# Unread matmuls in the planned gaps of TensorE behind the last scores of layer 2

## The chip, the cores and the metric

The kernel runs on one core of a Trainium2 chip. A core has TensorE (PE, matmuls; its weight loads are listed as PEld), VectorE (DVE), ScalarE (ACT), GpSimd (POOL), SyncE (SP, which here only issues DMAs) and 16 DMA engines. The metric is the device time of one execution in microseconds; lower is better. Everything is float32.

## The reference

Four layers are applied one after the other to x (4 sequences of 512 tokens, 256 channels). All four attend to the same context of 512 tokens.

```python
x = _L0_xattn_ref(x, ctx_1024, mask, ...)   # a Mamba-2 block, then cross attention, 8 heads of 32
x = _L1_xattn_ref(x, ctx_1024, ...)         # cross attention, 8 heads of 16, then an MLP
x = _L2_xattn_ref(x, ctx_1024, ...)         # layer norm, cross attention, 16 heads of 16, GELU
x = _L3_xattn_ref(x, ctx_1024, ...)         # cross attention, 8 heads of 32, then a recurrence
```

What ends the kernel is the recurrence of layer 3, which runs over all 512 tokens in order, for the four sequences at once:

```python
    U = (xn @ W_in.T + b_in) @ Bmat
    def step(s, u_t):
        s = jax.nn.silu(s @ A.T) + u_t          # s: 4 x 64
        return (s, s)
    _, states = jax.lax.scan(step, zeros, U.transpose(1, 0, 2))
    x = residual + einsum('tbs,sh->bth', states, Cmat)
```

## The kernel before

**Tiles.** The 512 tokens are cut into four tiles c = 0 to 3 of 128. A tile goes through layers 0, 1, 2 and 3, then through its 128 steps of the recurrence. Tiles overlap: while the recurrence of one runs, the attention of later tiles fills the engines. Layers 0 and 3 are the "wide" stream (tiles `kw`, `vw`, `probs_w`, `turned_w`), layers 1 and 2 the "slim" one (`ks`, `vs`, `probs_s`, `topped`). `slim_second` makes the last scores of layers 1 and 2 and their exponentials; when its loop over jobs ends, layers 1 and 2 have no scores left.

**Order.** No compiler orders the work. Each piece is a Python generator that yields operations, and `Flow.run` emits the one that can begin first by a table of estimated costs, in nanoseconds. `Engine.free` is when the plan has an engine free, `Flow.there(ops)` when the operands are there, `account` writes down ends of writes and reads. `Flow.emit` emits one operation, and `Flow.rows` the scores of up to two heads' groups in turns. The plan's times are not the chip's: an engine executes in the order emitted and waits on semaphores. All operations are emitted by one helper, so the profile gives line 119 for all of them.

**PSUM.** The tile `ps` has eight banks of 512 columns. `Banks.single` names the free bank that was read longest ago and does not reserve it; users take it out of the free set themselves. The recurrence owns bank 7 (`z`).

**The recurrence.** For each tile, one product puts the inputs into bank 7 (`u` by `amat`, 512 columns). Then every step adds the product of the previous result with `amat` (or `ahalf`, half of it) and reads it:

```python
            for t in range(P):
                if last is not None:
                    yield mm(z[:, t, :], last[0], last[1], False, True, skip_group_check=True)
                zt = z[0:SD, t, :]
                if exps["left"] == 0:
                    yield A.activation(r[0:SD, t, :], zt, AF.Silu)
                    last = amat, r[:, t, :]
```

The product has 65 rows, 65 weight columns (SZ = 65) and 4 streamed columns. A float32 matmul shows as two weight loads and two passes; a transpose as one. While exponentials are left (`exps["left"]`), a step takes two operations, a tanh on ScalarE and a multiply on VectorE; afterwards one SiLU on ScalarE, and ScalarE loads another table for it once. `output` multiplies the states by `cmat` (68 rows, 256 columns, once per sequence) and adds them to `h`. For the last tile it sends the result out one sequence at a time.

Of the kernel before, what the change touches and what calls it, by code (L numbers as in the profile page):

```python
# [28 lines left out]
SZ = SD + 1  # L29
# [14 lines left out]
def over(ap, n):  # L44

    p, a = ap.shape
    return ap.unsqueeze(1).to_broadcast([p, n, a])
# [8 lines left out]
DRAIN = 95.0  # L56
NEAR = 120.0
BOOST = 0.4
APART = 150.0
ALONE = 1500.0  # L60
WAIT = 400.0
# [23 lines left out]
class Op:  # L85
    def __init__(self, engine, name, args, kw):
        self.engine, self.name, self.args, self.kw = engine, name, args, kw
        outs = [kw["out"]] if "out" in kw else [args[0]]
        ins = list(args if "out" in kw else args[1:])
        ins += [v for k, v in kw.items() if k not in ("out", "accum_out")]  # L90
        ins = [v for v in ins if isinstance(v, bass.AP)]
        if kw.get("accum_out") is not None:
            outs.append(kw["accum_out"])
        self.writes = [b for ap in outs for b in blocks(ap)]
        self.reads = [b for ap in ins for b in blocks(ap)]
        self.size = max(elements(ap) for ap in outs + ins)
        self.mode = None
        self.table = None
        if engine.kind == "PE":
            lhs = kw.get("lhsT", ins[0])  # L100
            self.mode = tuple(next(m for m in (32, 64, 128) if n <= m)
                              for n in (lhs.shape[0], outs[0].shape[0]))
            n = max(elements(outs[0]), elements(lhs))
            self.cost = n / 1.2 * (1 if name == "transpose" else 2) + 5
        elif engine.kind == "DVE":
            each = {"reciprocal": 8.0, "scalar_tensor_tensor": 1.3}.get(name, 1.05)
            self.cost = 150 + self.size * each
        elif engine.kind == "ACT":
            self.cost = 165 + self.size * 0.83 + (190 if "accum_out" in kw else 0)
            f = args[2] if len(args) > 2 else None  # L110
            if f is not None and f not in NO_TABLE:
                self.table = f if f in OTHER_TABLE else "exp"
        elif engine.kind == "POOL":
            self.cost = 1000 if ALU.pow in args else 100 + self.size * 2.1
        else:
            self.cost = 500

    def emit(self):
        return getattr(self.engine.bass, self.name)(*self.args, **self.kw)  # L119
# [57 lines left out]
class Banks:  # L177
# [9 lines left out]
    def pair(self):  # L187
# [3 lines left out]
            two, default=None,  # L191
            key=lambda p: (max(self.at(p), self.flow.now) + APART * (p[1] > p[0] + 1), p),
        )

    def single(self):

        def key(i):
            beside = len({i - 1, i + 1} & self.free)
            return (max(self.at((i,)), self.flow.now) + APART * beside, i)

# [20 lines left out]
class Flow:  # L221
    def __init__(self):
        self.written, self.read = {}, {}
        self.threads = []
        self.now = 0.0
        self.landed = [0.0] * 8
        self.bus = 0.0

    def add(self, steps, urgency, name=""):
        th = Thread(steps, urgency, name)  # L230
# [67 lines left out]
    def account(self, ops, start, end):  # L298
        for op in ops:
# [3 lines left out]
            for b in op.reads:  # L303
                self.read[b] = max(end, self.read.get(b, 0.0))

    def emit(self, ops):

        for op in ops:
            e = op.engine
            start = max(e.free, self.there([op]))  # L310
            cost = op.cost
            if e.kind == "PE" and e.mode != op.mode:
                start, e.mode = start + DRAIN, op.mode
            if op.table is not None and e.table != op.table:
                cost, e.table = cost + TABLE, op.table
            end = start + cost
            e.free = end
            if e.kind == "DMA":
                start = max(start, min(self.landed))
                e.free = start + cost  # L320
                self.bus = max(self.bus, start + 2000) + op.size * P * 4 / 300
                self.landed[self.landed.index(min(self.landed))] = end = self.bus
            op.emit()
            self.account([op], start, end)

    def rows(self, threads, start):
        e = threads[0].choices[0][0].engine
        if e.mode != (32, 128):
            e.mode = (32, 128)
        built = []  # L330
        for th in threads:
            th.banks = th.request.take()
            th.request.banks.free -= set(th.banks)
            built.append(th.request.build(th.banks))
            start = max(start, th.request.banks.at(th.banks))
        for r in range(max(len(b) for b in built)):
            rounds = [b[r] for b in built if r < len(b)]
            for j in range(len(rounds[0])):
                for rnd in rounds:
                    rnd[j].emit()  # L340
        e.free = start + max(ROWS[t.request.kind] for t in threads)
        for b in built:
            self.account([op for rnd in b for op in rnd], start, e.free)
# [70 lines left out]
def tile_kernel(ctx: ExitStack, tc: tile.TileContext, a: dict, out: bass.AP):  # L414
# [6 lines left out]
    flow = Flow()  # L421
# [7 lines left out]
    def new(pool, name, *shape, dtype=F32):  # L429
        return pool.tile(list(shape), dtype, tag=name, name=name)  # L430
# [4 lines left out]
    def mm(dst, lhsT, rhs, start=True, stop=True, **kw):  # L435
        return T.matmul(dst, lhsT=lhsT, rhs=rhs, start=start, stop=stop, **kw)
# [23 lines left out]
    ps = new(ctx.enter_context(tc.tile_pool(name="ps", bufs=1, space=PSUM)), "ps", P, 8, S)  # L460
    banks = Banks(flow, ps.name, range(8))
# [47 lines left out]
    ident = new(common, "ident", P, P)  # L509
# [988 lines left out]
    def press(job, urgency):  # L1498
# [4 lines left out]
        if c == lead and not (l == 3 and rest):  # L1503
            urgency -= BOOST
        elif l == 0 and c > lead + 1:
# [120 lines left out]
    slim = Stream([], "s")  # L1626
# [48 lines left out]
    def slim_second(lo):  # L1675

        for i in range(slim.all):
            yield Until(lambda: len(slim_base) > i + 1)
            job = slim.order[i]
            for s in range(KL[job["l"]]):  # L1680
                n = slim_base[i] + s
                yield Until(lambda: n // 2 in slim_q2)
                p = yield take(f"probs_s{lo}")
                press(job, SECOND)
                q2, k = slim_q2[n // 2], job["k"][s // 2]
                pr = yield Row("second", (lo, lo + 1), banks, lambda pr: [
                    [
                        mm(
                            ps[:, pr[g], t * P : (t + 1) * P],
                            group(k[:, s % 2, t * P : (t + 1) * P], lo + g),  # L1690
                            group(q2[0][:, n % 2, :], lo + g),
                        )
                        for g in range(2)
                    ]
                    for t in range(NT)
                ])
                q2[1] -= 1
                if q2[1] == 0:
                    rings["topped"].give(q2[0])
                yield from read_both(pr, lambda i, sc: A.activation(p[:, i, :], sc, AF.Exp))  # L1700
                slim_probs[n, lo] = p
            slim.keys_read(job)

    def slim_weigh():

# [20 lines left out]
    def slim_finish(job, slot, c):  # L1726

        n = KL[job["l"]]
        r = wide_tops["rs", job["b"]]
        bank = yield on_bank(lambda bank: [  # L1730
            tr(ps[:, bank, j * P : (j + 1) * P], c[:, j, :]) for j in range(n)
        ])
        pt = ps[:, bank[0], 0 : n * P].rearrange("p (j t) -> p j t", j=n)
        yield V.reciprocal(
            r[:, 0 : 4 * n], pt.rearrange("p j (g r) -> p (j g) r", r=G)[:, :, 16]
        )
        banks.give(*bank)
        rb = yield take("rb")
        yield G_.tensor_copy(rb[:, 0 : 4 * n, :], along(r[:, 0 : 4 * n], G))
        ct_slot = yield take("ct")  # L1740
        ct = ct_slot[:, 0:n, :]
        bank = yield on_bank(lambda bank: [
            tr(
                ps[:, bank, j * P : (j + 1) * P],
                rb[:, 4 * j : 4 * j + 4, :].rearrange("p h r -> p (h r)"),
            )
            for j in range(n)
        ])
        pt = ps[:, bank[0], 0 : n * P].rearrange("p (j t) -> p j t", j=n)
        rings["rb"].give(rb)  # L1750
        yield V.tensor_tensor(ct, c, pt, ALU.mult)
        banks.give(*bank)
        rings["c"].give(slot)
        flow.add(job["after"](job["c"], job["b"], ct_slot, ct), CHAIN, f"from {job['l']} {job['c']}")


    def with_keys_made():
# [147 lines left out]
```

## Time and profile before

| what | value |
|---|---|
| median of 3 runs | 1499.82 us (1499.3 to 1504.79) |
| profiled execution | 1498.61 us, span 1496.9 us |
| PE busy | 1385.8 us (93%) |
| PEld busy | 998.1 us (67%) |
| DVE busy | 942.4 us (63%) |
| ACT busy | 759.7 us (51%) |
| granted clock of TensorE, mean | 0.933 |
| 1300.0 to 1370.0 us: PE busy, clock | 64.05 us, 0.88 |
| 1370.0 to 1380.3 us: PE busy, clock | 8.25 us, 0.67 |
| 1380.3 to 1486.6 us: PE busy, ACT busy, clock | 67.49 us, 26.54 us, 0.50 |
| 1486.6 to 1496.9 us: PE busy, clock | 4.88 us, 0.50 |

The page cuts the span into 40 slices of about 37 us and gives each engine's busy share in tenths; PEclk is the clock that TensorE was granted, in tenths of full speed. A row of the timeline has the start in us, the duration in us, the engine, the operation with its tiles (output, then inputs), its shape and how many instructions were merged; the bracket gives the idle time before it and what ended it. A row of a stretch has, after the stretch and its length, busy microseconds and instruction counts for PE, PEld, DVE, ACT and POOL, then the clock, then the share and rate of the DMA. Busy times of TensorE overlap and have modelled ends: they contain the time in which a result travels through the array.

### The profile page before, as it was taken

How to read it: one execution, taken by the hardware profiler on the slowest of the kernel's cores; microseconds unless marked ns; L12 is line 12 of the kernel's file. 1: busy time of each engine (PE TensorE's matmuls, PEld its weight loads, DVE VectorE, ACT ScalarE, POOL GpSimd, SP SyncE). 2: the span in 40 equal slices, each digit the busy share in tenths (PEclk: the TensorE clock that was granted, in tenths of full speed). 3: DMA queues.
4: the chain of work that ended last, by engine and by line, in shares of the span. 5: the costliest groups of instructions: out<-in, count | busy, mean ns of one | idle time of the engine just before them, and what ended most of it. 6: DMA issues, size and time to landing. Idle time of an engine off the chain costs nothing.

```text
span 1496.9 us, 34529 instructions
## 1 busy us (share of the span) xinstructions
PE 1385.8 (93%) x14432; PEld 998.1 (67%) x14432; DVE 942.4 (63%) x2079; ACT 759.7 (51%) x1904; POOL 257.2 (17%) x403
## 2 busy tenths in 40 slices
PE   7999998998999999999999999999999999998665
PEld 5667675675676667776767777676777666776443
DVE  5885878644866765687666767766676666655000
ACT  4643443332654565766456666454576544555221
POOL 2355555652010010100010100001100000010000
PEclk9999999997999999999999999998999999988555
DMA  7412011114432121233112122221222212010000
GB/s 226 138 43 87 29 53 29 65 59 134 141 102 85 63 74 52 97 100 103 60 61 74 52 94 94 68 88 46 75 80 82 84 61 89 11 48 1 14 1 14
DMA packets 48467, 107.59 MB, mean 72 GB/s; under 512 B 13044, under 2 KB 24760, under 8 KB 48312
## 3 DMA queue, kind: packets, MB, share of 16 engines
q1 hardware_dynamic: 46808, 105.32, 21.3%
q8 instruction: 113, 1.85, 0.5%
q10 hardware_dynamic: 1504, 0.07, 0.1%
q14 instruction: 42, 0.34, 0.1%
HBM read 85.01 MB, written 20.37 MB: 70 GB/s over the span
## 4 chain that ended last, share of the span: by engine, by line
PE 78%; DVE 10%; ACT 7%; issue 3%; DMA 1%; POOL 1%; SPq 0%; DVEq 0%; ACTq 0%; POOLq 0%
PE ps L119 78%; DVE tops L119 3%; ACT rec L119 2%; ACT probs_s L119 2%; DVE xbc L119 1%; DVE top L119 1%; DVE stats L119 1%; ACT xt L119 1%; DVE dt L119 1%; DVE probs_w L119 1%; DVE xt L119 1%; ACT probs_w L119 1%; ACT L119 1%; DMA w_out<-in_L_xattn_out_proj_w 0%; DMA ctx_in<-in_ctx 0%
## 5 line engine op out<-in xcount | busy, mean ns | idle before, releaser
L119 DVE TENSOR_REDUCE tops<-ps 128x2 f32<-128x1024 f32 (+1 forms) x214 | 235.0, 1107 | 68.6 <-PE ps L119 67.7
L119 ACT ACTIVATE probs_s<-ps 128x1024 f32<-128x1024 f32 (+1 forms) x210 | 193.6, 948 | 98.2 <-PE ps L119 93.5
L119 PE MATMUL ps<-ks,queries 32*128 32x512 f32 x768 | 197.1, 652 | 9.5 <-DVE tops L119 4.4
L119 PE MATMUL ps<-topped,ks 32*128 32x128 f32 x3072 | 183.2, 289 | 5.5 <-DVE rec L119 2.3
L119 PEld LDWEIGHTS ps<-topped,ks 32*128 32x128 f32 x3072 | 151.4, 190 | 31.6 <-issue 11.3
L119 PEld LDWEIGHTS ps<-rec,ahalf 65*65 65x65 f32 x694 | 76.6, 140 | 102.1 <-DVE rec L119 35.8
L119 PE MATMUL ps<-ident,probs_w 128*128 128x128 f32 x1024 | 139.6, 283 | 1.6 <-DVE tops L119 0.7
L119 PEld LDWEIGHTS ps<-ident,probs_w 128*128 128x128 f32 x1024 | 117.8, 146 | 17.7 <-issue 7.6
L119 ACT ACTIVATE rec_th<-ps 64x4 f32<-64x4 f32 x347 | 56.8, 164 | 139.8 <-PE ps L119 137.3
L119 PE MATMUL ps<-kw,queries 32*128 32x512 f32 x512 | 116.3, 644 | 3.3 <-ACT rec_th L119 1.0
L119 ACT COPY turned_w<-ps 128x512 f32<-128x512 f32 x154 | 86.9, 584 | 49.9 <-PE ps L119 39.7
L119 PE MATMUL ps<-probs_s,vs 128*32 128x128 f32 x3072 | 107.7, 282 | 0.7 <-DVE tops L119 0.4
L119 PE MATMUL ps<-rec,ahalf 65*65 65x4 f32 x694 | 93.4, 205 | 8.4 <-DVE rec L119 7.8
L119 ACT ACTIVATE probs_w<-ps,top 128x512 f32<-128x512 f32 x128 | 87.0, 683 | 23.5 <-DVE top L119 22.6
L119 PE MATMUL ps<-rec,amat 65*65 65x4 f32 x328 | 61.9, 259 | 39.8 <-ACT rec L119 39.8
L119 ACT ACTIVATE probs_w<-probs_w,top 128x512 f32<-128x512 f32 x128 | 91.4, 718 | 13.3 <-DVE top L119 13.3
L119 DVE CUSTOM_DVE_ANT_0 probs_w<-ps,masked 128x512 f32<-128x512 f32 x128 | 84.6, 682 | 18.4 <-PE ps L119 18.3
L119 PEld LDWEIGHTS ps<-probs_s,vs 128*32 128x32 f32 x3072 | 80.8, 112 | 17.7 <-issue 7.5
L119 DVE TENSOR_REDUCE top<-ps 128x2 f32<-128x1024 f32 (+1 forms) x70 | 78.4, 1127 | 19.8 <-PE ps L119 19.5
L119 DVE COPY turned_w<-ps 128x512 f32<-128x512 f32 x102 | 69.6, 688 | 28.6 <-PE ps L119 27.7
L119 PEld LDWEIGHTS ps<-rec,amat 65*65 65x65 f32 x328 | 49.0, 208 | 57.0 <-ACT rec L119 53.4
L119 PE MATMUL ps<-wo,ct 128*128 128x256 f32 x320 | 84.2, 395 | 2.8 <-DVE ct L119 1.8
(226 smaller groups left out, 2407.1 us busy)
## 6 DMA issues: line engine op xcount, KB each, us to landing
ks<-k SPq DMA_DIRECT2D x48, 512.0 KB, 4.5
kw<-k SPq DMA_DIRECT2D x32, 512.0 KB, 3.6
vw<-v SPq DMA_DIRECT2D x32, 512.0 KB, 3.5
k<-k_out SPq DMA_DIRECT2D x20, 512.0 KB, 2.6
vs<-v SPq DMA_DIRECT2D x16, 574.0 KB, 3.7
vs<-v SPq DMA_DIRECT2D x16, 302.0 KB, 2.9
v<-v_out SPq DMA_DIRECT2D x8, 512.0 KB, 2.6
v<-v_out SPq DMA_DIRECT2D x4, 574.0 KB, 2.9
```

The lines of the kernel that those rows point to most:

```text
L119: return getattr(self.engine.bass, self.name)(*self.args, **self.kw)
```

## The change

`Flow.fill` is called before TensorE's next operation is emitted, in `emit` and in `rows`. While the plan has TensorE free for more than GAP = 300 ns before that operation begins, it asks a filler for a matmul and emits it, if its planned end lies before that beginning. The filler is set when a `slim_second` thread has finished its last job; until then nothing is filled. It writes into the bank that `Banks.single` names, without taking it, and no operation reads what it writes. Its weights are 65 columns of the identity over all 128 rows; it streams up to 256 columns of the identity, as many as the gap of the plan has room for: (gap - 180) x 0.6.

```diff
+GAP = 300.0
...
+        self.filler = None
...
+    def fill(self, e, start):
+
+        while self.filler is not None and start - e.free > GAP:
+            op = self.filler(min(256, int((start - e.free - 180) * 0.3) * 2))
+            if op is None:
+                return
+            begin = max(e.free, self.there([op])) + DRAIN * (e.mode != op.mode)
+            if begin + op.cost > start:
+                return
+            e.mode, e.free = op.mode, begin + op.cost
+            op.emit()
+            self.account([op], begin, e.free)
+
     def emit(self, ops):
 
         for op in ops:
             e = op.engine
             start = max(e.free, self.there([op]))
+            if e.kind == "PE":
+                self.fill(e, start)
...
     def rows(self, threads, start):
         e = threads[0].choices[0][0].engine
+        self.fill(e, start)
...
             slim.keys_read(job)
+            if i == slim.all - 1:
+                flow.filler = filler
...
+    def filler(n):
+        bank = banks.single()
+        if bank is None:
+            return None
+        return mm(
+            ps[0:SZ, bank[0], 0:n].rearrange("p (i t) -> p i t", i=2), ident[:, 0:SZ],
+            over(ident[:, 0 : n // 2], 2),
+        )
```

## The prediction

> **What bounds the kernel now.** I read the page's slices first, then the chain that ended last, then stretches of the tail, then single steps in the timeline.
>
> ```profile
> PE   7999998998999999999999999999999999998665
> ...
> PEclk9999999997999999999999999998999999988555
> ```
>
> The last three of the 40 slices, about 112 us, run at half the TensorE clock, and TensorE is only 50 to 60% busy there. Nothing is left then but the recurrence of layer 3, whose steps depend on each other. The chain of waits alternates there between TensorE and ScalarE, with no DMA and no VectorE in it. One step at full clock (just before the clock falls at 1380.3 us) and one at half clock:
>
> ```profile
> 1379.12 0.28 PE L119 MATMUL ps<-rec,amat 65*65 65x4 f32 x2 [0.26 <-ACT rec L119]
> 1379.66 0.28 PE L119 MATMUL ps<-rec,amat 65*65 65x4 f32 x2 [0.26 <-ACT rec L119]
> ...
> 1408.07 0.38 PE L119 MATMUL ps<-rec,amat 65*65 65x4 f32 x2 [0.26 <-ACT rec L119]
> 1408.71 0.38 PE L119 MATMUL ps<-rec,amat 65*65 65x4 f32 x2 [0.26 <-ACT rec L119]
> ```
>
> From start to start it is 0.54 us at full and 0.64 us at half clock. The 0.17 us ACTIVATE and the hand-overs are equal in both; the 0.10 us lies in the two weight loads and passes. So the tail is bound by a latency in which the clock is the only soft part.
>
> **What sets the clock.** It changes at multiples of 3.41 us. In each such stretch I counted how long matmul passes stream through the array: passes x columns x 0.84 ns at full, 1.67 ns at half clock. These come from four passes of 256 columns, the last of which takes about 0.25 us longer to drain:
>
> ```profile
> 1362.37 1.13 PE L119 MATMUL ps<-wo,ct 128*128 128x256 f32 x4 [0.17 <-DVE ct L119]
> ...
> 1385.63 1.97 PE L119 MATMUL ps<-xt,wub 128*64 128x256 f32 x4
> ```
>
> (1.13 - 0.25)/4 = 0.22 us, (1.97 - 0.25)/4 = 0.43 us. Four pairs of neighbouring stretches; the column after POOL is the clock, and the second line of a pair has what was granted after the first:
>
> ```profile
> 1335.85:1339.26 3.41, 2.33 (x20) 1.98 (x20) 2.36 (x12) 2.33 (x9) 1.53 (x4) 1.00 0.00 0
> 1339.26:1342.68 3.42, 3.27 (x48) 2.72 (x46) 1.01 (x4) 0.78 (x3) 0.89 (x1) 1.00 0.29 96
> 1376.81:1380.22 3.41, 2.38 (x23) 1.68 (x15) 2.03 (x8) 0.84 (x5) 0.00 (x0) 0.99 0.00 0
> 1380.22:1383.63 3.41, 2.38 (x14) 2.03 (x15) 0.85 (x3) 0.83 (x5) 1.03 (x3) 0.51 0.00 0
> 1311.95:1315.37 3.42, 3.42 (x25) 3.40 (x26) 1.59 (x4) 2.48 (x5) 0.00 (x0) 0.50 0.00 0
> 1315.37:1318.78 3.41, 3.41 (x47) 2.67 (x49) 0.75 (x4) 1.57 (x5) 0.29 (x1) 0.50 0.00 0
> 1349.50:1352.92 3.42, 3.42 (x15) 2.41 (x13) 2.14 (x4) 1.75 (x7) 0.00 (x0) 0.51 0.01 2
> 1352.92:1356.33 3.41, 3.41 (x50) 2.42 (x51) 2.23 (x6) 2.12 (x7) 0.29 (x1) 0.99 0.00 0
> ```
>
> PE busy does not tell them apart (2.33 stays warm, 2.38 falls), the streaming share does. From 1335.85: 13 transposes of 0.109 us = 1.42 us, 0.40: stays. From 1376.81: four passes of 256 and eight quarter-array passes, 0.30: falls. Over all stretches, at full clock every fall has 0.36 or less and every stay 0.385 or more; at half clock every rise has 0.73 or more, every other 0.70 or less. A pass over 32 rows counts a quarter, and over 68 rows about half (cmat<-s_aug from 1404.16 streams 0.76 of its stretch and the clock stays low). Do columns count too? Only the pair from 1349.50 speaks: eight transposes (0.50) and the 64-column passes of wub (0.33, half if columns count). It rises. As rows alone it has 0.84; with columns counted 0.67, less than the 0.70 from 1311.95 that does not rise. So I take it that rows count and columns don't. This is one stretch, and the forecast rests on it.
>
> **The change part by part.** The order of the instructions of both programs shows nothing moved: VectorE, ScalarE, GpSimd and the DMA queue keep theirs, and TensorE gets 169 matmuls of 128 rows x 65 columns: 12 between 1336 and 1373 us (76 to 256 streamed columns), 28 of 142 columns in the third tile of the recurrence from about 1374, 123 of 142 in the fourth, and six at the joints and the end.
>
> *The fill in a full-clock step.* Two loads of 65 columns (0.055 us each) and two passes of 142 (0.119 us each): 0.24 us of streaming. Counted from the recurrence's second pass, the fill has left the array at 0.30 us; the next step's load is released at 0.43. It is hidden with 0.13 us to spare. If that cover went, each step would cost what exceeds it.
>
> *Will the clock hold?* 0.24/0.54 = 0.44 of the array, over the 0.385 that held. Two rules of the Trainium skill differ. "TensorE: Matmul & The Clock Gate", section "HAM oscillation", asks for no idle gaps over about 3.4 us. The gaps here are 0.26 us and the clock is 0.50 for 116 us; by that rule the fill changes nothing (0 us), by the rows it is what was missing. The same page's "Back-to-back issue gap" gives N/2.4 + 2.5 ns per warm matmul: two passes of 142 would be 0.12 us, 0.23 of a step, the clock would fall and the fill would only cost. The row (0.22 us for 256 columns) has nearly double that; the measured row decides. The joint of the tiles has no fills: one 512-column product over 65 rows (0.85 us x 0.51) and four cmat (0.43 us x 0.53 each) in about 3.3 us are 0.41: holds, narrowly.
>
> *Sum of the tail at full clock.* Third tile from 1380.3: 23 plain steps x 0.102 = 2.4, the steps beside ln, xt and wub 1.8: 4.2 us. Joint: the 512-column product 0.9, four steps beside cmat from 1.18 to 0.60: 3.1 us together. Fourth tile: 123 x 0.102 = 12.5 us. End: four times two passes at 0.22 for 0.43 and one load: 2.1 us. Together -21.9 us.
>
> *The 12 early fills.* They lift the stretches from 1346.1 (0.29) and 1366.5 (0.33) by 0.27 and 0.42, so the cold spells after them (3.4 and 6.8 us) go. These stream 7.4 us at half clock; at most 3.7 us come back, none if ScalarE or VectorE bound them all; about half of the stretch waits for those: -2.0.
>
> *Added waits.* Seven fills wait for the reader of their bank. One of 76 columns, amid the ln transposes at 1347, waits for an exponential; three transposes and the next recurrence step queue behind it: at most +0.5 us. The 744 columns at 1368 wait for ct and leave about 0.1 us late; the first of 142 at 1374 waits for a copy, up to +0.3. Elsewhere the reader is done. Together +0.8 (0 to +1.5). Fetching the added instructions: the instruction queues take 0.6% of the DMA engines; I put it at nothing, with 1 us the other way if the fetch shows.
>
> Net: -21.9 - 2.0 + 0.8 = -23.1. The profiled execution has 1498.61 us (span 1496.9): 1475.5. The median stands 1.2 above it: 1476.7, say 1477; own range 1472 to 1486.
>
> **The rivals.**
>
> *Columns count: the clock falls again, and the fill is pure load (slower).* A full-clock step then has 0.22, under 0.36, and the tail goes cold within two stretches. At half clock the fill's loads and passes last 0.108 + 2 x 0.237 us, and the recurrence's second load 0.108 follows before its second pass: 0.69 to 0.70 us per step, above the 0.64 that the latency needs. The trace has the pattern: with cmat between steps (load 0.21, passes 0.85, load 0.11) they are 1.18 apart, at 1404.13 and 1405.31. About 145 steps x 0.056 = +8 us, +0.5 at the end, early part 0 to -1.2: 1508. It decides where a fill's share falls under 0.36. For it: few stretches with narrow passes exist. Against: the rise after 1349.50.
>
> *The clock holds until the joint and not after it.* 0.41 is near the limit, and once cold a filled step streams 0.47/0.696 = 0.68, below the 0.73 of the lowest rise: it would not come back. Gains of the third tile and before -5.4, cost of the fourth 123 x 0.056 + 0.5 = +7.4: 1502.
>
> *The fills do too little* (the page's gap rule): 1500, with no mechanism in the trace for it.
>
> **How the numbers follow.** Clock held to the end: 0.62. Columns count: 0.22. Lost at the joint: 0.10. The rest, 0.06, is a clock that alternates, around 1490. The prediction is the first case's, 1477. Its own range leaves too much out, so the range reaches from 1472 to 1507, into the second and third cases. A difference under 0.5% (7.5 us) can't be told from no change here. Faster by more (below 1492.3): 0.62 and most of the alternating clock, 0.67. Within: the joint case and part of the columns case, 0.17. Slower by more: 0.16.
>
> **What would show it.** PEclk 9 or 10 in the last slices, steps of 0.54 us with a fill between, ACT's idle time unchanged: right. PEclk 5 with steps of 0.70: columns count. A change from 0.54 to 0.70 at the cmat products: the joint. Steps between 0.56 and 0.62 at full clock would say that the fill's cover was mis-sized. If the clock was held and the stretch before 1370 us came out longer, the early waits were too cheap in my sum.

## The result, and the profile after

The changed kernel takes 1499.43 us (median of 14 runs, 1496.55 to 1506.68), the kernel before 1499.32 us on the same chips (14 runs). The ratio is 1.0003, 95% interval 0.9986 to 1.0021: no difference that can be measured, where 1477 us was forecast. The profiled execution took 1498.39 us (before 1498.61), with a span of 1496.7 us (before 1496.9). Its TensorE rows of the slices:

```profile
PE   7999998997999999999999999999999999999999
...
PEclk9999999997999999999999999999999999889555
```

TensorE is now busy to the end, as the change wants, and the clock still falls to half in the last three slices. Stretches show where it falls (the columns are as in the prediction: stretch, length, busy time and count of PE, PEld, DVE, ACT and POOL, then the clock, then the DMA):

```profile
1376.30:1379.70 3.40, 3.40 (x28) 2.11 (x26) 1.28 (x5) 1.15 (x7) 1.03 (x3) 1.00 0.00 0
1379.70:1383.10 3.40, 2.46 (x17) 1.52 (x16) 0.78 (x2) 1.12 (x5) 0.00 (x0) 1.00 0.00 0
1383.10:1386.50 3.40, 3.40 (x22) 2.69 (x23) 0.00 (x0) 0.83 (x5) 0.00 (x0) 0.52 0.00 0
...
1485.50:1489.00 3.50, 3.50 (x19) 2.64 (x18) 0.38 (x1) 0.72 (x5) 0.00 (x0) 0.50 0.00 0
1489.00:1492.40 3.40, 3.24 (x15) 1.79 (x13) 1.01 (x3) 0.00 (x0) 0.00 (x0) 0.99 0.14 46
```

In the tail the clock falls once, at 1383.2 us, after a stretch in which PE was busy for 2.46 of 3.40 us. It comes back once, at 1489.1, after the last step. The timeline (start, duration, engine, operation; the bracket is the idle time before it) shows the stretch at fault:

```profile
1379.74 0.28 PE L120 MATMUL ps<-rec,amat 65*65 65x4 f32 x2
1380.03 0.56 ACT L120 ACTIVATE xt<-ps,beta,g 128x256 f32<-128x256 f32 x1 [0.35 <-DVE xt L120]
...
1380.70 0.28 PE L120 MATMUL ps<-rec,amat 65*65 65x4 f32 x2 [0.69 <-ACT rec L120]
...
1380.91 1.08 PE L120 MATMUL ps<-xt,wub 128*64 128x256 f32 x4
...
1381.92 0.28 PE L120 MATMUL ps<-rec,amat 65*65 65x4 f32 x2
...
1382.63 0.46 PE L120 MATMUL ps<-ident 128*65 128x142 f32 x2
```

Between 1379.74 and 1382.63 no fill was emitted, while xt is made and the inputs `u` of the next tile are projected (xt by wub). The plan of the changed kernel, worked through, has gaps there: 432 ns before the second of these steps and 418 ns before the last, both over GAP. What it refuses is the bank. The one that `Banks.single` names comes free only 214 and 410 ns into the gap, so the planned end of the fill would lie behind the start of the step. (Around wub itself the plan has no gap.) What streams there is four passes of wub (4 x 256 x 0.84 ns = 0.86 us) and one fill (0.24): 1.10 us of 3.41, 0.32. Before that stretch and after it a filled step looks like this:

```profile
1376.49 0.28 PE L120 MATMUL ps<-rec,amat 65*65 65x4 f32 x2
1376.63 0.44 PE L120 MATMUL ps<-ident 128*65 128x142 f32 x2
1377.03 0.28 PE L120 MATMUL ps<-rec,amat 65*65 65x4 f32 x2
...
1389.13 0.33 PE L120 MATMUL ps<-rec,amat 65*65 65x4 f32 x2
1389.32 0.72 PE L120 MATMUL ps<-ident 128*65 128x142 f32 x2
1389.83 0.33 PE L120 MATMUL ps<-rec,amat 65*65 65x4 f32 x2
```

At full clock the fill is hidden: 0.54 us from step to step, as without it. At half clock it is load: 0.69 to 0.70 us (0.693 on average), where the plain step of before took 0.64. So the time went in a circle. Against before, the first SiLU step starts 2.2 us earlier (1371.33 for 1373.54). Of these, 0.3 us are there ahead of the first fill (at the exponential that starts at 1335.38 in the kernel before, 1335.06 here); 1.9 are the early fills'. The third tile gains another 2.8 us (the `u` product starts at 1396.05 for 1401.02), nearly all before the clock falls: wub starts 9.6 us behind the first SiLU step, before 12.1. The end gains 1.8 from the clock that came back. The fourth tile loses 6.6 us: 123 filled steps, each 0.053 us longer. Together -0.2 us.

### The profile page after: what moved, and what is told of

Same layout as the page of the kernel before. It is cut to its first block, busy times and chain, and to the rows that moved or that the text cites. A ratio compares the mean times of both kernels' runs of the same rounds, so it can differ in the third digit from the quotient of the medians.

```text
span 1496.7 us, 35205 instructions
## 1 busy us (share of the span) xinstructions
PE 1429.4 (96%) x14770; PEld 1036.6 (69%) x14770; DVE 941.7 (63%) x2079; ACT 759.9 (51%) x1904; POOL 257.3 (17%) x403
## 4 chain that ended last, share of the span: by engine, by line
PE 81%; DVE 10%; ACT 5%; issue 2%; POOL 1%; DMA 0%; DVEq 0%; ACTq 0%; POOLq 0%
PE ps L120 81%; DVE tops L120 2%; ACT probs_s L120 2%; DVE xbc L120 1%; DVE top L120 1%; DVE stats L120 1%; ACT probs_w L120 1%; ACT L120 1%; ACT xt L120 1%; DVE dt L120 1%; DVE probs_w L120 1%; DVE xt L120 1%; POOL h L120 0%; DMA ctx_in<-in_ctx 0%; ACT turned_w L120 0%
## 5 line engine op out<-in xcount | busy, mean ns | idle before, releaser
L120 PE MATMUL ps<-ident 128*65 128x142 f32 (+4 forms) x338 | 111.6, 443 | 0.3 <-ACT turned_w L120 0.2
L120 ACT ACTIVATE probs_w<-ps,top 128x512 f32<-128x512 f32 x128 | 87.0, 683 | 23.4 <-DVE top L120 22.6
L120 PEld LDWEIGHTS ps<-ks,queries 32*128 32x128 f32 x768 | 57.3, 186 | 41.1 <-DVE tops L120 9.7
```

## The experiments

In what follows the share of a stretch is the time in which passes stream, over 3.41 us; "by rows" weights it with the occupied rows (65 or 68 of 128 count about half), "by cells" with the occupied columns as well. A share is good to about 0.03: it changes by up to that much when the stretch is taken 0.1 us earlier or later. Every time is a median, with the kernel before on the same chip beside it.

Two theories stand against each other for the missing gain. A: the share by rows sets the clock, 142 columns are too few to come back with once the clock has fallen, and it fell beside xt and wub, in a stretch without fills. B: the fills can't hold the clock, because narrow weights (65 columns) hardly count, or they cost more than they bring.

**A longer fill.**

```diff
-            op = self.filler(min(256, int((start - e.free - 180) * 0.3) * 2))
+            op = self.filler(min(256, int((start - e.free - 180) * 0.4225) * 2))
```

Behind a step the fill then has 200 columns; some of the early fills get longer too.

> The fills of the recurrence stream 200 columns instead of 142 (the factor in the gap's formula is raised), still with 65 weight columns. My theory (rows count, columns don't; the changed kernel lost the clock in the stretch from 1379.7 us, where three steps have no fill and the share by rows is 0.32, and could not come back because a filled half-clock step streams only 0.69 to 0.70, below the lowest rise of 0.73): a half-clock step of 0.11 + 2 x 0.33 + 0.11 = 0.88 us streams 0.75, so the clock returns within one or two stretches of 3.4 us after each fall; steps of 0.54 us nearly everywhere in the fourth tile; 1480 to 1486 us. The rival (columns count): a full-clock step has 0.62 x 0.51 = 0.32 and falls, a half-clock step 0.38 and never rises: 145 steps at 0.88 instead of 0.64, about 1530 us.

1479.95 us (4 runs; before 1499.02, ratio 0.9852, 0.9804 to 0.9901).

```profile
1380.40:1383.80 3.40, 2.46 (x18) 1.56 (x17) 0.73 (x2) 1.12 (x5) 0.00 (x0) 1.00 0.00 0
1383.80:1387.20 3.40, 3.40 (x19) 2.48 (x18) 0.00 (x0) 0.67 (x4) 0.00 (x0) 0.51 0.00 0
1387.20:1390.60 3.40, 3.40 (x28) 2.06 (x27) 0.00 (x0) 1.00 (x6) 0.00 (x0) 0.99 0.02 5
```

The clock falls in the same place (share by rows 0.35), and is back one stretch later: a filled half-clock step of 0.887 us streams 0.74 to 0.75 by rows. By cells that stretch has 0.38, little more than half of what a cold stretch of the kernel before has without rising (0.67, from 1311.95 us), so the count by cells can't be what decides. At the joint the clock fell again (0.36) for three stretches, 10 us. The more expensive fill is worth 19 us where the cheaper one is worth nothing: this is against B.

**A fill behind every step.** In this kernel the fill is emitted with the step itself, and the plan's gaps are not filled while SiLU steps run. The four steps beside cmat in the fourth tile stay without one:

```diff
+                    step = mm(z[:, t, :], last[0], last[1], False, True, skip_group_check=True)
+                    if exps["left"] == 0 and not (c == NT - 1 and t < 4):
+                        step.tail = 142
+                    yield step
...
+            if op.tail and self.filler is not None:
+                self.filler(op.tail).emit()
```

> A fill of 142 columns directly behind every SiLU step of the recurrence, whatever the plan says, except the four steps beside cmat in the fourth tile; the order of all other work is that of the kernel before, and the early fills stay. My theory (the unfilled stretch beside xt and wub lost the clock): that stretch goes from 0.32 to about 0.53 and the clock holds; if it also holds at the joint of the tiles (0.41 by my count) the result is 1476 to 1480 us, if it falls there the fourth tile runs at 0.69 us per step and the result is about 1498. The rival (columns count, or the fill's identity data is not seen as activity): the clock falls within two stretches of 1376 us as in the changed kernel: 1499 to 1503.

1498.7 us (20 runs; ratio 0.9995, 0.9977 to 1.0013). The hole is closed (the first line, 0.53 by rows, keeps the clock), and the clock then falls at the joint of the tiles:

```profile
1380.30:1383.70 3.40, 3.40 (x29) 2.28 (x29) 1.09 (x4) 1.00 (x6) 1.03 (x3) 1.00 0.00 0
1397.40:1400.80 3.40, 3.35 (x14) 1.46 (x14) 0.76 (x2) 0.50 (x3) 0.00 (x0) 1.00 0.00 0
1400.80:1404.20 3.40, 3.40 (x16) 2.71 (x16) 1.30 (x4) 0.52 (x4) 0.00 (x0) 0.51 0.00 0
```

The stretch from 1397.4 holds a fill, the 512-column `u` product and the first two of the four cmat products. PE is busy nearly throughout, but over 65 and 68 rows: 0.32 by rows. From there on the steps take 0.69 to 0.70 us to the end. So there are two holes, and with 142 columns either is enough to lose all that follows.

**The same with 200 columns** (`step.tail = 200`).

> As e2_every_step, but with 200 columns. My theory: holds everywhere or comes back after a fall at the joint within two stretches; a full-clock step hides 0.06 + 0.33 = 0.39 us of fill before the next load is released at 0.43, so steps stay at 0.54: 1475 to 1481. The rival (columns count): about 1530.

1481.31 us (4 runs; ratio 0.9854, 0.9811 to 0.9897). The clock falls at the joint (0.385) and is back after two stretches (the second had 0.79 by rows, 0.40 by cells). No better than the first longer fill, though the stretch beside xt and wub is warm here: steps beside turned, wo and wub are filled too and get longer (1.61, 1.32 and 1.61 us for 1.22, 1.04 and 1.22). From the first SiLU step to the last `u` product it is 23.4 us, with the first longer fill 23.3, so this cost eats the whole gain of the warm stretch. Fills where the engine isn't waiting have a price.

**The early fills alone** (the filler gives nothing once the exponentials are done):

```diff
-        if bank is None:
+        if bank is None or exps["left"] == 0:
```

> Fills only while exponentials are left (10 fills, none in the SiLU steps). It measures the early fills by themselves: the changed kernel begins its first SiLU step 2.2 us earlier than the kernel before, so about -2 us, 1497; the tail at 0.64 us per step as before. If the early gain came from something else than the fills, no difference.

1495.63 us (12 runs; ratio 0.9970, 0.9943 to 0.9996), 3.4 us under before. The interval reaches from -0.6 to -8.5 us. The profiled run is one of 1506.44 us, but its trace shows where that comes from: it loses 8 us between 360 and 500 us, in spells of half clock (13.7 us each, from 405.7 and from 460.3), long before the first fill. Taken from the exponential named above, its first SiLU step comes after 36.3 us (changed kernel 36.3, before 38.2) and its end after 157.7 us (changed kernel 161.6, before 161.5). So the early fills by themselves bring 1.9 us up to the first SiLU step and 3.8 us up to the end, since the tail then begins at full clock, and the later fills of the changed kernel give all of it back.

**More rows, no other change.** The changed kernel with its 142 columns, and six tiles padded with zero rows:

```diff
-    cmat = new(common, "cmat", SD + B, D)
+    cmat = new(common, "cmat", P, D)
+    nc.gpsimd.memset(cmat[SD:], 0.0)
-    amat = new(common, "amat", SZ, SZ)
+    amat = new(common, "amat", P, SZ)
...
-            us[i], rs[i] = new(pool, f"u{i}", SZ, B, P + 1), new(pool, f"rec{i}", SZ, P, B)
+            us[i], rs[i] = new(pool, f"u{i}", P, B, P + 1), new(pool, f"rec{i}", P, P, B)
...
-        w["s_aug"] = s_aug = new(pool, "s_aug", SD + B, B, P)
+        w["s_aug"] = s_aug = new(pool, "s_aug", P, B, P)
```

(`ahalf` likewise.) Nothing in the order of TensorE changes.

> The changed kernel with its fills unaltered (142 columns); amat, ahalf, cmat, u, rec and s_aug get 128 rows instead of 65 or 68, the added ones zero. No instruction, no column and no order on TensorE changes. Theory (occupied rows x time decides the clock): up to the joint as the changed kernel (the clock falls at the stretch beside xt and wub, filled steps of 0.69-0.70 us). At the joint the u product then streams 1.71 us over all rows at half clock and four cmat 0.855 us of each 1.18: a stretch of 0.75 or more, so the clock comes back there, the fills (0.44) hold it, and the fourth tile's steps are 0.54 instead of 0.694 us: 119 x 0.153 = -18 us, cmat steps another -1.5: about 1479 us (1476 to 1484). Rival (zero rows don't count, or columns and not rows count): nothing changes, 1499 us, clock 0.5 and 0.694 us to the end.

1479.65 us (4 runs, 1476.23 to 1486.98; before 1500.41; ratio 0.9869, 0.9841 to 0.9896). In the profiled execution (1477.35 us) the clock is 1.0 throughout the tail:

```profile
1380.10:1383.60 3.50, 3.50 (x29) 2.30 (x28) 1.42 (x4) 1.00 (x6) 1.03 (x3) 1.00 0.00 0
1383.60:1387.00 3.40, 2.46 (x17) 1.53 (x16) 0.49 (x2) 1.19 (x6) 0.00 (x0) 1.00 0.00 0
1387.00:1390.40 3.40, 3.40 (x27) 1.90 (x25) 0.00 (x0) 1.10 (x7) 0.00 (x0) 1.00 0.00 0
...
1397.20:1400.60 3.40, 3.40 (x17) 1.76 (x15) 0.84 (x2) 0.50 (x3) 0.00 (x0) 1.00 0.00 0
```

The joint (last line) now has 0.55 by rows and holds; by cells it has 0.47. The size is as expected, but in part by luck: the clock was expected to fall beside xt and wub and to come back at the joint, and here it did not fall at all. The same operations straddle the 3.41-us stretches otherwise (wub starts 0.9 us into its stretch, 1.2 us in the changed kernel), and the poorest one had 0.38. Other runs of this kernel took 5 to 10 us longer, with mean clocks of 0.966 and 0.968 for 0.973; they have no trace. They may have lost the clock beside xt and wub, or lost time before the tail, as the run of 1506.44 us above did; which of the two is not shown.

**Control: the padding without fills** (the kernel before, with the same six tiles).

> Control: the kernel before, without any fill, with the six tiles at 128 rows (the added ones zero). Theory: the padding itself moves no instruction; without fills the clock still falls about 1377-1380 us and a plain step streams 0.01 of the array, so it stays at half clock. Only the joint is richer (u product and four cmat over all rows: about 0.8 of one or two stretches), so the clock comes back there for one or two stretches: -0.5 to -2.5 us, 1497 to 1499.5 us. Rival (the gain of the padded kernels has another source than the fills being held warm): 1480 here as well.

1499.52 us (20 runs; before 1501.06; ratio 0.9991, 0.9978 to 1.0004). The padding alone brings nothing that can be measured. Its joint had stretches of 0.64 and 0.73 to 0.75 by rows at half clock, and the clock did not come back there, though that had been expected for one or two stretches.

**Fewer rows.** The 200-column fill over 65 rows:

```diff
-            ps[0:SZ, bank[0], 0:n].rearrange("p (i t) -> p i t", i=2), ident[:, 0:SZ],
-            over(ident[:, 0 : n // 2], 2),
+            ps[0:SZ, bank[0], 0:n].rearrange("p (i t) -> p i t", i=2), ident[0:SZ, 0:SZ],
+            over(ident[0:SZ, 0 : n // 2], 2),
```

> The kernel with the 200-column fill, the fill over 65 rows instead of 128 (same columns, loads, passes and order). Theory (rows count): a filled full-clock step has 0.34 us x 0.51 of 0.535 = 0.32, below 0.36: the clock falls in the third tile, a filled half-clock step has 0.67 x 0.51 of 0.885 = 0.39, far below 0.73: it never comes back, and each of some 140 steps takes 0.885 us: about 1526 us (1518 to 1534). Rival (only that the array streams counts, however many rows): as with 128 rows, 1480.

1529.31 us (one run; before 1500.41). Order, loads, passes and columns are those of the 1480-us kernel. Two stretches after the fall:

```profile
1384.50:1387.90 3.40, 3.40 (x18) 2.48 (x18) 0.00 (x0) 0.67 (x4) 0.00 (x0) 0.51 0.00 0
1387.90:1391.30 3.40, 3.40 (x17) 2.58 (x16) 0.00 (x0) 0.67 (x4) 0.00 (x0) 0.50 0.02 5
```

The first of them has nearly the numbers of the second line of the longer fill above (PE 3.40, PEld 2.48, clock 0.51), and there the clock rose after it; here it doesn't. By rows it has 0.38 instead of 0.74. Steps stay at 0.887 us to the end. With the padded kernel this shows from both sides that the rows of the array that a pass occupies count. The rises at 0.376 to 0.40 by cells speak against columns, and so does the full clock: the padded kernel held it with 0.20 by cells beside xt and wub, where the kernel before lost it at 1370.1 us after 0.34. No run changed the columns of the weights alone.

**How long must the fill be?** 170 columns (factor 0.359), 65-row recurrence as in the changed kernel:

> The changed kernel with 170 streamed columns in place of 142, 65 rows in the recurrence as in the changed kernel. The clock falls beside xt and wub as before. A filled half-clock step is then 0.787 us (0.694 + 28 x 2 x 1.67 ns) with 0.575 us of streaming: 0.73, between the 0.70 that does not rise and the 0.737 to 0.74 that did. If the limit is below 0.73: the clock comes back and the time is 1480 to 1487. If it is above: cold to the end, 140 steps x 0.093 = +13: about 1511 us.

1476.93 us (one run; before 1501.06).

```profile
1380.70:1384.10 3.40, 2.46 (x17) 1.48 (x16) 0.81 (x2) 1.14 (x6) 0.00 (x0) 1.00 0.00 0
1384.10:1387.50 3.40, 3.40 (x20) 2.80 (x20) 0.00 (x0) 0.69 (x5) 0.00 (x0) 0.51 0.00 0
1387.50:1390.90 3.40, 3.40 (x18) 2.68 (x18) 0.00 (x0) 0.82 (x5) 0.00 (x0) 0.50 0.02 5
1390.90:1394.30 3.40, 3.40 (x28) 2.03 (x26) 0.00 (x0) 1.00 (x6) 0.00 (x0) 0.98 0.00 0
```

It falls in the same place, stays cold for one stretch more than with 200 columns (0.71 to 0.74), then rises (0.74). The count can't tell these two stretches apart. The joint, at 0.354, kept the clock here; with 200 columns and no padding it lost it at 0.357. So at full clock the edge lies about 0.36, and the count doesn't say which way it goes there. One execution can't say how often 170 columns are enough.

**Both cures together.** Padding with 200 columns; the same with a fill between two steps that have nothing else between them; and that with 142 columns. The last two:

```diff
+                if op.step and self.bare and self.filler is not None:
+                    self.filler(self.bare).emit()
+                self.bare = op.step
```

> The kernel with the 200-column fill, with the same six tiles at 128 rows. Theory (rows): the joint, 0.36 of its stretch before, gets the other half of the u product (0.85 x 0.49 us) and of the cmat products: about 0.5, so the clock holds through it; the cold spell of 10 us at the joint goes (-4 us), and the one after the last step too (-1). One cold stretch stays, beside xt and wub (0.35). About 1475 us (1473 to 1478). Rival (columns or data): as the kernel with the 200-column fill, 1480, with the clock lost at the joint.

1476.27 us (5 runs, 1474.53 to 1476.53; before 1500.41; ratio 0.9836, 0.9821 to 0.9850). The joint holds at 0.54 by rows; one cold stretch is left beside xt and wub (0.36).

> As the kernel before it here, and a 200-column fill also between two SiLU steps that have nothing else between them (7 fills, three of them beside xt and wub). Theory: the stretch beside xt and wub rises from 0.35 to over 0.45 and the clock is 1.0 from the first SiLU step to the end: another -1 us: 1474 us (1472 to 1477), mean clock 0.98. If the fills beside xt and wub delay xt or wub, the same time as without them.

1475.89 us (4 runs; ratio 0.9837, 0.9823 to 0.9851). The cold stretch is gone (0.45 by rows), and the time is the same within its spread: four steps of 0.887 us in place of 0.54 are worth 1.4 us.

> The changed kernel with its 142-column fill, the six tiles at 128 rows, and a 142-column fill also between two SiLU steps that have nothing else between them. Theory: no stretch of the tail is left under 0.385 (beside xt and wub about 0.42, joint over 0.5, filled steps 0.44), so the clock is 1.0 from the first SiLU step to the end: 1476 us (1474 to 1479), the same as with 200 columns, and without the spread that the padded kernel had without the added fills (1476 to 1487). Rival (142 columns are too few, 200 are needed): over 1485.

1475.36 us (4 runs, 1474.16 to 1480.45; before 1501.06; ratio 0.9828, 0.9796 to 0.9860), mean clock 0.975. Its clock in the slices:

```profile
PEclk9999999997999999999999999999999999989999
```

The stretch beside xt and wub, that of the joint, and one of the added fills:

```profile
1380.80:1384.20 3.40, 2.33 (x15) 1.43 (x14) 0.91 (x2) 1.08 (x5) 0.00 (x0) 1.00 0.00 0
...
1394.50:1397.90 3.40, 3.30 (x15) 1.51 (x14) 0.61 (x2) 0.50 (x3) 0.00 (x0) 1.00 0.00 0
...
1381.89 0.46 PE L121 MATMUL ps<-ident 128*65 128x142 f32 x2 [0.63 <-ACT rec L121]
```

142 columns are enough, if no stretch is left thin. The stretch beside xt and wub is held only narrowly, 0.37 and not the 0.42 expected: the fills added there come late, as the plan of the changed kernel foresaw (the one shown starts after 0.63 us of idle time, ended by ScalarE). This is the lowest time here, with the two above within its spread. With the same fill it is at 0.9828 of before, where the changed kernel is at 1.0003.

## Why the prediction was wrong

**The step that failed is "Will the clock hold?".** It asked whether filled steps hold the clock (0.44: yes, and they do) and whether the joint does (0.41). It didn't ask for every stretch of the tail. The one from 1379.70, with 0.32, was missed: the sum has "the steps beside ln, xt and wub" as a gain of 1.8 us, as if the clock held there, while the fills of these steps were refused for their bank. The order of the instructions shows it: four SiLU steps with wub as the only thing between them. In place of a held clock the runs show 106 us at half clock, with steps of 0.693 us.

**The joint's 0.41 was mis-sized too.** Measured were 0.32, 0.36 and 0.385 in stretches of three kernels that lost the clock there, and 0.354 in one that didn't. The sum had the `u` product and four cmat in about 3.3 us. At full clock they take 4.2 us (with 170 columns from 1396.46, the start of the `u` product, to 1400.63, where the last cmat pass has streamed), and the same streaming over 4.2 us is 0.32 and not 0.41. Besides, the stretches of the clock lie differently on the program from run to run (wub 0.9 or 1.2 us into its stretch, above), and one can hold the `u` product with its waits and only one or two of the cmat. With the first hole closed, the second took over (a fill behind every step: 1498.7 us).

**The limit of 0.385 was read too sharply.** The prediction has every fall at 0.36 or less and every stay at 0.385 or more. Counted again, the trace of before has 0.36 for the stretch from 1288.1 us, which stays warm, and 0.37 for the stretches before the falls at 349.5 and 557.7 us. A share of 0.41 at the joint was thus no safe distance.

**The rival that lost the clock at the joint had the mechanism, not the place.** Its sentence that a filled half-clock step streams 0.68, below the lowest rise, and so never comes back, is what the fourth tile shows (0.69 to 0.70 for over 100 us). It was applied to the joint alone, with a chance of 0.10; it holds for any hole. The sign set down for the other rival, half clock with steps of 0.70 us for "columns count", came true without it: a cold filled step takes that long whatever made the clock fall.

**What was right.** Rows count and columns don't: the forecast rested on one stretch, and the fills of 65 and of 128 rows and the zero rows now show it. The hidden fill: 0.54 us with and without it. The cold step: 0.69 to 0.70 forecast, 0.693 measured. Early fills with their waits and third tile: -5.4 together forecast, -4.7 measured (1.9 up to the first SiLU step, 2.8 behind it); end: -2.1 and -1.8. Joint and fourth tile: -15.6 forecast, +6.6 measured; these 22.2 us are nearly all of the miss. And the sum for a held clock, 1477, is near what the profiled runs that hold it through the tail took (1475.5 to 1477.4).

The Trainium skill's rule that was weighed there ("TensorE: Matmul & The Clock Gate", "HAM oscillation": no idle gaps over about 3.4 us) decides nothing here. In the changed kernel the clock is 0.50 for 106 us in which PE shows no idle time, and 28 more columns per fill or zero rows end that. Of these 106 us:

```profile
1460.00:1480.00 20.00, 20.00 (x118) 16.47 (x116) 0.37 (x1) 4.84 (x29) 0.00 (x0) 0.50 0.00 0
```

The share of the stretch separates the cases.

Left open: what exactly separates a fall from a hold between 0.354 and 0.385, and why one run of the last kernel took 1480.45 us (cold spells before the tail, as in the run of 1506.44 us, would do it; it has no trace).

## What to carry to other kernels

Before work is added to hold a clock, list the share of every stretch in which it must hold, the thin ones first: the state is kept by the poorest stretch, not by the mean. Give the filler enough to come back with at half clock, or it turns into load at the first hole. And where a product occupies half of the rows anyway, zero rows raise its share at no cost in time that was measurable here (ratio 0.9991 without fills).

## What was not expected of the hardware

In these traces the clock has two thresholds far apart, in the share by rows over 3.41 us. In the tails it fell at 0.385 and less and held at 0.354 and more (both happened between). It rose above 0.75 and stayed low at 0.70 and less; at 0.71 to 0.75 both happened (the kernel before rose at 1376.9 us after 0.73, the padded control did not after 0.73 to 0.75). So the same filled step can run at either clock to the end: the 142-column fill keeps the full clock with 0.44 and can't leave the half clock with 0.70, and the 24 us between 1499 and 1475 hang on one or two stretches of 3.4 us. Zero rows count as well: the joint held with them (0.55) where 142-column fills without them lost it (0.32).
